# Router and seam of a two-layer graph network with 16 experts: gates from two logits, expert owners ahead of slots, six tiles of weights, square root after block 14

## The chip, the cores and the metric

The kernel runs on one core of a Trainium2 chip. The metric is the device time of the kernel in microseconds (us); of several runs the median counts. The core has five engines that run their own instruction streams in order and meet at semaphores: PE (TensorE, matrix products), DVE (VectorE), ACT (ScalarE), POOL (GpSimd) and SP (SyncE, which here only issues transfers). SP, ACT and POOL issue DMA transfers, which 16 DMA engines carry out.

## The reference, cut to what matters

3125 nodes of 256 features pass four steps, each a layer norm, an operator and a residual: a graph attention with 8 heads, a mixture of 16 experts (top 2), a graph attention of three layers, and a feed-forward block that treats part of the rows. The change lies in the second step:

```python
logits = jnp.einsum('bsd,de->bse', x, gate_w) + gate_b
probs = jax.nn.softmax(logits, axis=-1)
top_probs, top_idx = jax.lax.top_k(probs, 2)
top_probs = top_probs / jnp.sum(top_probs, axis=-1, keepdims=True)
dispatch = jnp.sum(jax.nn.one_hot(top_idx, n_experts, dtype=x.dtype) * top_probs[..., None], axis=-2)
h1 = jnp.einsum('bsd,edh->bseh', x, w1)
h2 = jnp.einsum('bsd,edh->bseh', x, w2)
hidden = jax.nn.silu(h1) * h2
expert_out = jnp.einsum('bseh,eho->bseo', hidden, w3)
return jnp.einsum('bseo,bse->bso', expert_out, dispatch)
```

Since the two probabilities are divided by their sum, the gates of a node depend on the difference of its two best logits alone: with d = second − first, the first gate is 1/(1+exp d) and the second exp d/(1+exp d).

## The kernel before, in words

Nodes lie in NB = 25 blocks of P = 128 (NP = 3200 rows with padding), in NCH = 5 chunks of CH = 5 blocks (CW = 640 rows). All is float32 unless a tile says bfloat16.

**First attention** (to about 980 us). For every chunk, head and source block ACT and DVE make a masked weight matrix, and PE multiplies it (L593, L612). The last chunk's end flows into the seam.

**The seam** (980 to 1056 us). What it does, in order:
- Generators in `endings` and `stats` finish the last chunk; `stats` ends with a square root on ACT (L654) and a reciprocal on DVE (L655), and `rows` makes the five normed blocks b20 to b24 (L660, DVE).
- The router goes over the 25 blocks. PE transposes the normed block (L813), ACT copies it from PSUM (L816), and PE multiplies it by `gate_w` (L818) into one PSUM tile of logits. Inside `tc.manual_schedule` DVE and ACT run in the order in which the code names them, so the place of each call is its place in the queue. After b9 stand the square root and the rows; after b9, b19 and b24 `choice` finds the best two experts of the blocks so far with 13 DVE operations (L775 to L782) behind one that adds the bias (L828). After b15 and b23 `gates` turns the logits of the 10 chosen blocks into gates (L787 to L799: an exponential on ACT and 12 DVE operations) and SP writes them to columns D and D+1 of `xn_d` (L800).
- For the first six transfers of later weights (`later_weights`, L844 and L846) ACT is the issuing engine.
- PE sums the chosen experts over nodes (`ptot`, `pin`, L877, L879). DVE makes running sums (`pre`, L886 to L890), the number of tiles of each expert (`tiles`), their ends (`end`), and from these the place of each pair of node and expert (`where`, `place`, `part`, L905 to L922). From `part` come one-hot tiles `slot` and `give` (L932, L937), which PE multiplies (`pslot`) into a list: for each of the 64 expert tiles, which 128 node-expert pairs stand in it.
- Between these, the last five blocks' gates are finished (L790 to L800); then `owner`, the expert of each tile, is made by a comparison of 1024 elements (`which`, L948), a sum (`own`, L950) and a minimum (L951). `token` (row to gather, L964) and `target` (row to add to, L967) come last.

**The experts** (1056 to 1428 us). MU = 56 tiles run always, up to 8 more if the count needs them. For tile i, SP reads `owner[i]` into a register and loads that expert's w1, w2, w3 (512 KB each, L985, L987, L989); these are in a pool `ew0` of three buffers. POOL gathers 128 rows of `xn_d` with their gates (`xg`, L991). PE transposes them, multiplies by w1 and w2 (L1000), ACT and DVE form `hid` (L1004, L1005), PE multiplies by w3 (`po`, L1008), DVE scales by the gate (`yo`, L1014), and POOL adds the rows into `x_d` with an indirect transfer (L1015). Each of these adds waits until the one before has landed.

**After the experts** ACT loads `x` from `x_d` in five transfers (L1030). POOL issues, in its queue's order, `wr`, `br` (L1046, L1048), the two feed-forward matrices `fw1` and `fw2` of 1 MB each (L1056, L1058) and `fb2` (L1061). The feed-forward bias `b1` (4 KB, 8 x 128) is loaded by POOL into a tile named `rjunk` (L1111), transposed on PE (L1113) and copied by DVE (L1114); a scheduler, not the code's order alone, decides where POOL and PE get these, and the rooms of tiles decide with it. Then DVE and ACT norm the rows (`lengths`, L1126 to L1135; L1143) and PE makes features (L136, L1098).

**The second attention** (1494 to 2402 us) is a long chain of PE products (L1345); its `at<-adj` mask loads (L1330, three of 800 KB at first) are issued ahead by SP. The feed-forward block ends the kernel.

Transfers issued by SP and ACT share eight semaphore lanes; a transfer waits for the one before it on its lane.

Of the kernel before, what the change touches and what calls it, by code (L numbers as in the profile page):

```python
# [13 lines left out]
OP = mybir.AluOpType  # L14
# [70 lines left out]
def network(ctx: ExitStack, tc: tile.TileContext, ins, out, flag):  # L85
# [464 lines left out]
    with tc.tile_pool(name="m0a", bufs=1) as ap, tc.tile_pool(name="m0", bufs=2) as mp, tc.tile_pool(  # L550
# [118 lines left out]
        made, state = [], {}  # L669
        evictions, endings = [], []  # L670
        load(0, range(NCH))
        for u in range(len(units) + LEAD0):
            if u == H * NB:
                nc.scalar.dma_start(gate_w, ins["L0_ffn_gate_w"].rearrange("(k p) e -> p k e", p=P))
                nc.scalar.dma_start(gate_b, spread(ins["L0_ffn_gate_b"], NE))
            if u < len(units):
                dc, h, s = units[u]
                if h == H - 1 and s == 0 and dc + 1 < NCH:
                    load(dc + 1, range(NCH - 1))
                made.append(produce(dc, h, s, state))  # L680
            if u < LEAD0:
                continue
            dc, h, s = units[u - LEAD0]
            if h == 0 and s == 0:
                red = mp.tile([P, H, 2 * CH, C1], F32, name="red", bufs=1)
                total = mp.tile([P, CH, H, C1], F32, name="total")
                others = shared(dc, total)
            if s == 0:
                acc = ps.tile([P, 3, 512], F32, name="acc")
            consume(dc, h, s, made.pop(0), acc)  # L690
            for _ in range(2 if s % 4 == 3 else 1):
                next(others, None)
            if s == NB - 1:
                evictions.append((u + LEAD0, dc, h, acc, red))
                if h % 4 == 3:

                    while next(others, None) == h // 4:
                        pass
                    steps = [finish(dc, red, total, h // 4)]
                    if h == H - 1 and dc < NCH - 1:  # L700
                        steps.append(stats(dc))
                    if h == H - 1 and dc == NCH - 2:
                        steps += [rows(g) for g in range(NCH - 1)]
                    endings += [(u + LEAD0 + 2, e) for e in steps]
                    if h == H - 1 and dc + 1 < NCH:

                        load(dc + 1, [NCH - 1])
            if evictions and u >= evictions[0][0]:
                evict(*evictions.pop(0)[1:])
            if endings and u >= endings[0][0] and u % 2 and next(endings[0][1], None) is None:  # L710
                endings.pop(0)
# [52 lines left out]
        t3, l2, ex = [room_of_x(ex3, F32) for _ in range(3)]  # L764
# [19 lines left out]
        def gates(bs, ex, t3):  # L784

            e = ex[:, bs]
            nc.vector.tensor_sub(e, lg[:, bs], across(best[0], bs))  # L787
            nc.scalar.activation(e, e, AF.Exp)
            yield
            nc.vector.tensor_reduce(den[:, bs], e, AX.X, OP.add)  # L790
            nc.vector.reciprocal(den[:, bs], den[:, bs])
            nc.vector.tensor_mul(e, e, across(den, bs))
            for i in range(2):
                nc.vector.tensor_mul(t3[:, bs], e, one_hot[i][:, bs])
                nc.vector.tensor_reduce(gate[:, bs, i], t3[:, bs], AX.X, OP.add)
            nc.vector.tensor_add(den[:, bs], gate[:, bs, 0], gate[:, bs, 1])
            nc.vector.reciprocal(den[:, bs], den[:, bs])
            for i in range(2):
                nc.vector.tensor_mul(gate[:, bs, i], gate[:, bs, i], den[:, bs])  # L799
            nc.sync.dma_start(xn_d[bs.start * P : bs.stop * P, D:].rearrange("(b p) c -> p b c", p=P),  # L800
                                gate[:, bs])
        with tc.manual_schedule(engines={mybir.EngineType.DVE, mybir.EngineType.Activation}):
# [5 lines left out]
            logits = ps.tile([P, 3, 512], F32, name="acc")[:, 0, : NB * NE].rearrange("p (b e) -> p b e", e=NE)  # L808
            done = 0
            for b in range(NB):  # L810
# [5 lines left out]
                nc.scalar.copy(xt[:, : 2 * P], pt[:, : 2 * P])  # L816
                for k in range(2):
                    nc.tensor.matmul(logits[:, b, :], xt[:, k * P : (k + 1) * P], gate_w[:, k, :],  # L818
                                     start=(b == 0 and k == 0), stop=(k == 1), skip_group_check=True)
                if b in (9, 19, NB - 1):  # L820
                    if b == 9:

                        for e in (ends[-1], rows(NCH - 1)):
                            for _ in e:
                                pass
                    bs = slice(done, b + 1)
                    done = b + 1
                    nc.vector.tensor_add(lg[:, bs, :], logits[:, bs, :],  # L828
                                         gate_b[:, None, :].to_broadcast([P, done - bs.start, NE]))
                    choice(bs, t3, l2)  # L830
                if b in (15, 23):
                    giving = gates(bs, ex, t3)
                    next(giving)
                    next(giving, None)
# [26 lines left out]
    with tc.tile_pool(name="mo", bufs=1) as mo:  # L861
# [7 lines left out]
        with tc.tile_pool(name="mg", bufs=1) as mg, tc.tile_pool(name="mg1", bufs=1, space=PSUM) as ps1, tc.manual_schedule(  # L869
# [11 lines left out]
            giving = gates(slice(20, NB), ex, t3)  # L881
            next(giving)

# [19 lines left out]
            end = running(tiles, mg.tile([P, NE], F32, name="end0"), mg.tile([P, NE], F32, name="end1"), NE)  # L903
            base = mg.tile([P, NE], F32, name="base")
# [19 lines left out]

            pslot = ps1.tile([P, 2, MT], F32, name="pslot")
            pairs = lambda t: t.rearrange("p (q e) -> p q e", e=2)[:, :, None, :]
            for i in range(2):
# [17 lines left out]
            which = mg.tile([P, MT, NE], F32, name="which")  # L945
            nc.gpsimd.iota(which, pattern=[[1, MT], [0, NE]], base=0, channel_multiplier=0,
                           allow_small_or_imprecise_dtypes=True)
            nc.vector.tensor_tensor(which, which, end[:, None, :].to_broadcast([P, MT, NE]), OP.is_ge)  # L948
            own = mg.tile([P, MT], F32, name="own")
            nc.vector.tensor_reduce(own, which, AX.X, OP.add)  # L950
            nc.vector.tensor_scalar(owner, own, float(NE - 1), None, op0=OP.min)  # L951

# [16 lines left out]
        def experts(first, last, ew):  # L969

            with tc.tile_pool(name="ep", bufs=2, space=PSUM) as ps:
                w3_loads = []
                for i in range(first, last):
# [10 lines left out]
                    w1 = ew.tile([P, 2, HID], F32, name="w1")  # L984
                    nc.sync.dma_start(w1, ins["L0_ffn_w1"][ds(e, 1)].rearrange("o (k p) h -> p (o k) h", p=P))  # L985
                    w2 = ew.tile([P, 2, HID], F32, name="w2")
                    nc.sync.dma_start(w2, ins["L0_ffn_w2"][ds(e, 1)].rearrange("o (k p) h -> p (o k) h", p=P))  # L987
                    w3 = ew.tile([P, HID // P, D], F32, name="w3")
# [31 lines left out]
        experts(0, MU, ew0)  # L1020
        early.close()
        count = nc.values_load(used[0:1, 0:1], min_val=0, max_val=MT)
        with tc.If(count > MU):
            with tc.tile_pool(name="ew2", bufs=2) as ew:
                experts(MU, MU + 2, ew)
            with tc.If(count > MU + 2):
                with tc.tile_pool(name="ew3", bufs=3) as ew:
                    experts(MU + 2, MT, ew)
# [1146 lines left out]
```

## Time and profile before

| what | us |
|---|---|
| median of 3 runs | 2539.43 |
| the runs | 2529.86, 2539.43, 2539.63 |
| profiled execution, its own time | 2538.2 |
| span of the profiled execution | 2536.3 |
| PE busy in it | 2199.5 (87%) |
| DVE busy | 1553.2 (61%) |
| ACT busy | 1286.6 (51%) |
| POOL busy | 194.9 (8%) |

The span lies 1.9 us under the execution's own time. A row of a timeline reads: start, length, engine, line, operation, tiles out<-in, shape, count, and in brackets how long the engine had been idle and what it waited for. A row of windows reads: stretch, its length, busy time of each engine with its instructions, the granted share of the TensorE clock, the mean busy share of the 16 DMA engines, and what they moved in GB/s. An engine name with q (SPq, POOLq) means the issuing of a transfer.

### The profile page before, as it was taken

The page shows a single profiled execution, that of the slowest core. Times are in us where ns is not written, and L with a number is a line of the kernel's source. Part 1 is how long each engine was busy: PE and PEld are TensorE (multiplying, and loading weights), DVE is VectorE, ACT ScalarE, POOL GpSimd, SP SyncE. Part 2 cuts the span into 40 slices and gives each one's busy share as a digit, 9 for nine tenths or more (in the row PEclk, how much of TensorE's full clock was granted, in tenths as well). Part 3 has the DMA queues.
Part 4 walks back from the last instruction along what each step waited for, and adds up shares of the span by engine and source line. Part 5 has one row for each costly group of instructions (what it writes and reads, how often), then busy time and mean ns, then how long its engine had stood idle before and what let it go on. Part 6 is the DMA issues. An engine that isn't in the chain of part 4 may idle for free. (4 is left out here: it accounts for less than half of the span.)

```text
span 2536.3 us, 38394 instructions
## 1 busy us (share of the span) xinstructions
PE 2199.5 (87%) x15049; PEld 1872.8 (74%) x15049; DVE 1553.2 (61%) x2978; ACT 1286.6 (51%) x1804; POOL 194.9 (8%) x182
## 2 busy tenths in 40 slices
PE   2526699999999998499999589999899998999997
PEld 1325568888888887488888468888788887888765
DVE  6699979999999997532222334444344443677851
ACT  1364479999999895011111154444444445444321
POOL 2000000000000000233443200000000000000021
PEclk9755599999999998699999799999999999999999
DMA  3005430202020211699999412222122221444330
GB/s 88 12 23 192 130 114 22 92 25 95 22 97 22 66 43 34 205 305 297 279 277 290 130 55 71 71 83 76 58 71 80 73 72 59 107 109 97 70 83 18
DMA packets 155547, 260.80 MB, mean 103 GB/s; under 512 B 12938, under 2 KB 99481, under 8 KB 155353
## 3 DMA queue, kind: packets, MB, share of 16 engines
q1 hardware_dynamic: 127187, 211.13, 26.7%
q0 software_dynamic: 13440, 22.80, 4.3%
q10 hardware_dynamic: 14726, 24.27, 3.3%
q8 instruction: 123, 2.02, 0.3%
q14 instruction: 71, 0.58, 0.1%
HBM read 211.60 MB, written 46.57 MB: 102 GB/s over the span
## 5 line engine op out<-in xcount | busy, mean ns | idle before, releaser
L1345 PE MATMUL bcc<-hx,r 128*128 128x257 f32 x3750 | 840.0, 383 | 13.4 <-DVE r L1336 13.4
L1345 PEld LDWEIGHTS bcc<-hx,r 128*128 128x128 f32 x3750 | 710.9, 191 | 113.0 <-DVE r L1336 13.7
L586 ACT ACTIVATE t<-row,steep 128x640 bf16<-128x640 f32 x800 | 592.4, 817 | 59.2 <-DVE m L588 38.3
L593 PE MATMUL acc<-parts,m 128*128 128x198 bf16 x5000 | 575.3, 247 | 4.6 <-DVE m L588 3.7
L1336 DVE SCALAR_TENSOR_TENSOR r<-t,colc,at 128x640 f32<-128x640 f32 x375 | 329.5, 882 | 397.9 <-PE bcc L1345 384.3
L1334 ACT ACTIVATE t<-rowb,colm,cola 128x640 f32<-128x640 f32 x375 | 341.9, 919 | 387.0 <-DVE r L1336 386.4
L593 PEld LDWEIGHTS <-m 128*128 128x128 bf16 x5000 | 442.2, 96 | 101.7 <-DVE m L588 17.0
L612 PE MATMUL all<-parts,at 128*128 128x396 bf16 x1250 | 366.4, 337 | 6.1 <-DVE total L614 3.8
L588 DVE TENSOR_TENSOR m<-t,at 128x1280 bf16<-128x1280 bf16 x400 | 327.3, 820 | 39.6 <-ACT t L586 31.8
L1000 PEld LDWEIGHTS h<-xT,w 128*128 128x128 f32 x1792 | 214.1, 194 | 17.5 <-ACT xT L138 14.4
L1000 PE MATMUL h<-xT,w 128*128 128x128 f32 x1792 | 219.1, 279 | 7.8 <-ACT xT L138 7.7
L529 PE MATMUL pa<-oh,ol 128*128 128x100 bf16 (+1 forms) x1120 | 94.7, 277 | 111.9 <-DVE oh L522 111.9
L579 DVE SCALAR_TENSOR_TENSOR m<-row,nleft,at 128x640 bf16<-128x640 f32 x200 | 174.7, 874 | 10.5 <-DMA adj<-cnt 8.0
L529 PEld LDWEIGHTS <-ol 128*128 128x128 bf16 x1120 | 87.0, 141 | 119.5 <-DVE oh L522 62.0
L1004 ACT ACTIVATE hid<-h 128x512 f32<-128x512 f32 x56 | 33.4, 597 | 261.0 <-PE h L1000 256.1
L1014 DVE TENSOR_SCALAR yo<-po,share 128x256 f32<-128x256 f32 x56 | 27.1, 484 | 203.0 <-DMA x_d<-yo,target 123.8
L612 PEld LDWEIGHTS <-at 128*128 128x128 bf16 x1250 | 119.2, 98 | 16.2 <-issue 10.7
L1008 PE MATMUL po<-w,hid 128*128 128x256 f32 x448 | 113.2, 396 | 18.5 <-DVE hid L1005 18.4
L532 ACT CAST cnt<-pa 128x2000 bf16<-128x2000 f32 x40 | 73.0, 1826 | 82.8 <-PE pa L529 82.8
L138 ACT COPY xT<-pt 128x256 f32<-128x256 f32 x158 | 56.0, 375 | 107.1 <-PE pt L136 104.0
L1008 PEld LDWEIGHTS po<-w,hid 128*128 128x128 f32 x448 | 82.0, 193 | 35.2 <-DVE hid L1005 22.5
L1015 POOL DMA_INDIRECT x_d<-yo,target x56 | 89.5, 1599 | 213.4 <-DVE share L1010 121.9
(410 smaller groups left out, 1740.6 us busy)
## 6 DMA issues: line engine op xcount, KB each, us to landing
w<-in_L_ffn_w_dram SPq DMA_DIRECT2D x168, 512.0 KB
at<-adj SPq DMA_DIRECT2D x100, 800.0 KB
adj<-cnt SPq DMA_DIRECT2D x10, 2000.0 KB
row<-er_d ACTq DMA_DIRECT2D x40, 320.0 KB
xf_d<-hx SPq DMA_DIRECT2D x5, 1282.5 KB
right<-rr_d ACTq DMA_DIRECT2D x15, 320.0 KB
x_d<-x SPq DMA_DIRECT2D x5, 640.0 KB
xn_d<-at SPq DMA_DIRECT2D x5, 640.0 KB
```

The costliest lines, as they stand in the source:

```text
L529: nc.tensor.matmul(pa[:, q // NW, p0 + c0 : p0 + c1], hot[0][:, q // 2, :, q % 2], hot[1][:, q // 2, c0:c1, q % 2], start=(u == 0), stop=( ...
L579: nc.vector.scalar_tensor_tensor(m, row, nleft[:, s, h : h + 1], at[:, k, :], op0=OP.is_ge, op1=OP.mult)
L586: nc.scalar.activation(t[:, int(i), :], row, AF.Relu, bias=steep[:, s, h : h + 1], scale=STEEP)
L588: nc.vector.tensor_tensor(m, t, at[:, k - 1 : k + 1, :], OP.min)
L593: nc.tensor.matmul(acc[:, db // 2, db % 2 * C6 : (db % 2 + 1) * C6], m[:, db * P : (db + 1) * P], parts[:, s, h, :], start=(s == 0 and db ...
L612: nc.tensor.matmul(alone, at, parts[:, s, hs, 3 * C1 :], start=(s == 0), stop=(s == NB - 1))
L1000: nc.tensor.matmul(ph[:, f, :], w[:, k, f * P : (f + 1) * P], xt[:, k, :], start=(k == 0), stop=(k == 1))
L1008: nc.tensor.matmul(po, hid[:, f, :], w3[:, f, :], start=(f == 0), stop=(f == HID // P - 1))
L1015: nc.gpsimd.indirect_dma_start(out=x_d, out_offset=bass.IndirectOffsetOnAxis(ap=target[:, i : i + 1], axis=0), in_=yo, in_offset=None, com ...
L1334: nc.scalar.activation(t, rowb[:, dw], AF.Relu, bias=colm[:, s : s + 1], scale=cola[:, s : s + 1])
L1336: nc.vector.scalar_tensor_tensor(r, t, colc[:, s : s + 1], at[:, s % CH, :], op0=OP.add, op1=OP.mult)
L1345: nc.tensor.matmul(accs[dc][db][:, : D + 1], r[:, db * P : (db + 1) * P], hx[:, s, : D + 1], start=(s == 0), stop=(s == NB - 1))
```

## The change

Four edits meet in the seam.
- **Router.** Two steps (b0 to b14, b15 to b24) in two PSUM banks take the place of three in one; square root and rows stand after b14 instead of b9.
- **Gates.** `gates` goes. The exponential of the difference of the two best logits is taken once for all 25 blocks; an addition, a reciprocal and a product follow once `part` is made, and ACT writes all gates in one transfer of 3200 pieces of 8 bytes.
- **Owners.** `used`, `which`, `own` and `owner` stand right behind `end`, ahead of `base`.
- **Weights.** w1, w2, w3 get six buffers each.

```diff
-            logits = ps.tile([P, 3, 512], F32, name="acc")[:, 0, : NB * NE].rearrange("p (b e) -> p b e", e=NE)
-            done = 0
+            logits = ps.tile([P, 3, 512], F32, name="acc")
+            steps = (0, 15, NB)
...
-                if b in (9, 19, NB - 1):
-                    if b == 9:
-                        for e in (ends[-1], rows(NCH - 1)):
+                if b == 14:
+                    for e in (ends[-1], rows(NCH - 1)):
...
-                if b in (15, 23):
-                    giving = gates(bs, ex, t3)
-                    next(giving)
-                    next(giving, None)
+            nc.vector.tensor_sub(den, best[1], best[0])
+            nc.scalar.activation(gate[:, :, 1], den, AF.Exp)
...
-            giving = gates(slice(20, NB), ex, t3)
-            next(giving)
...
             end = running(tiles, mg.tile([P, NE], F32, name="end0"), mg.tile([P, NE], F32, name="end1"), NE)
+            nc.vector.tensor_copy(used, end[:, NE - 1 :])
+            which = mg.tile([P, MT, NE], F32, name="which")
...
+            nc.vector.tensor_scalar(owner, own, float(NE - 1), None, op0=OP.min)
             base = mg.tile([P, NE], F32, name="base")
...
             nc.vector.tensor_copy(part[:, :, :, :NB], part_i)
+            nc.vector.tensor_scalar(den, gate[:, :, 1], 1.0, None, op0=OP.add)
+            nc.vector.reciprocal(gate[:, :, 0], den)
+            nc.vector.tensor_mul(gate[:, :, 1], gate[:, :, 1], gate[:, :, 0])
+            nc.scalar.dma_start(xn_d[:, D:].rearrange("(b p) c -> p b c", p=P), gate)
...
-            next(giving, None)
-            nc.vector.tensor_copy(used, end[:, NE - 1 :])
...
-            nc.vector.tensor_scalar(owner, own, float(NE - 1), None, op0=OP.min)
             second = mg.tile([P, MT], F32, name="second")
...
-                    w1 = ew.tile([P, 2, HID], F32, name="w1")
+                    w1 = ew.tile([P, 2, HID], F32, name="w1", bufs=deep)
...
-        experts(0, MU, ew0)
+        experts(0, MU, ew0, 6)
```

The diff also hands the tiles `red` and `total` of the first attention out from a function; the stream of instructions there stays the same. Outside the diff the scheduler places two things anew, as the built order of instructions shows: `at<-adj` (three loads on SP) stands amid the experts' weight loads instead of ahead of them, and `rjunk` (POOL) stands behind `fw1`, `fw2` and `fb2` instead of among the first gathers, so that PE's transpose of it and DVE's copy of it come first on PE, and ahead of the reciprocal L1130 on DVE, after the experts.

More of the change, by code (lines that the diff above doesn't have):

```diff
@@ L669, in network, with sums_of @@
         made, state = [], {}
+        def sums_of(dc):
+            return mp.tile([P, H, 2 * CH, C1], F32, name="red", bufs=1), mp.tile([P, CH, H, C1], F32, name="total")
+        red, total = sums_of(0)
         evictions, endings = [], []
@@ L684, in network @@
             if h == 0 and s == 0:
-                red = mp.tile([P, H, 2 * CH, C1], F32, name="red", bufs=1)
-                total = mp.tile([P, CH, H, C1], F32, name="total")
+                if dc:
+                    red, total = sums_of(dc)
                 others = shared(dc, total)
@@ L763, in network @@
         nc.vector.tensor_copy(tritb, trit)
-        t3, l2, ex = [room_of_x(ex3, F32) for _ in range(3)]
+        t3, l2 = [room_of_x(ex3, F32) for _ in range(2)]
         assert taken[0] <= (NCH - 1) * CH * D
@@ L782, in choice @@
             nc.vector.tensor_mul(chosen[:, bs], chosen[:, bs], across(real, bs))
[L784 to L801, printed above, removed]
         with tc.manual_schedule(engines={mybir.EngineType.DVE, mybir.EngineType.Activation}):
@@ L903, in network @@
             end = running(tiles, mg.tile([P, NE], F32, name="end0"), mg.tile([P, NE], F32, name="end1"), NE)
+            nc.vector.tensor_copy(used, end[:, NE - 1 :])
+            which = mg.tile([P, MT, NE], F32, name="which")
+            nc.gpsimd.iota(which, pattern=[[1, MT], [0, NE]], base=0, channel_multiplier=0,
+                           allow_small_or_imprecise_dtypes=True)
+            nc.vector.tensor_tensor(which, which, end[:, None, :].to_broadcast([P, MT, NE]), OP.is_ge)
+            own = mg.tile([P, MT], F32, name="own")
+            nc.vector.tensor_reduce(own, which, AX.X, OP.add)
+            nc.vector.tensor_scalar(owner, own, float(NE - 1), None, op0=OP.min)
             base = mg.tile([P, NE], F32, name="base")
@@ L941, in network @@
                                      start=(i == 0 and b == 0), stop=(i == 1 and b == NB - 1))
-            next(giving, None)
-            nc.vector.tensor_copy(used, end[:, NE - 1 :])
[L945 to L951, printed above, removed]
             second = mg.tile([P, MT], F32, name="second")
@@ L967, in network, with experts @@
             nc.vector.scalar_tensor_tensor(target, number, -1.0, none2, op0=OP.add, op1=OP.add)
-        def experts(first, last, ew):
+        def experts(first, last, ew, deep):
             with tc.tile_pool(name="ep", bufs=2, space=PSUM) as ps:
@@ L1024, in network @@
             with tc.tile_pool(name="ew2", bufs=2) as ew:
-                experts(MU, MU + 2, ew)
+                experts(MU, MU + 2, ew, 2)
             with tc.If(count > MU + 2):
                 with tc.tile_pool(name="ew3", bufs=3) as ew:
-                    experts(MU + 2, MT, ew)
+                    experts(MU + 2, MT, ew, 3)
         for g in range(NCH):
```

23 lines of the change are left out of this document (13 added, 10 removed).

## The prediction

> **What bounds the kernel now.** First I read the busy rows by windows around the seam.
>
> ```profile
> 975.00:990.00 15.00, 13.31 (x119) 11.25 (x116) 10.06 (x25) 3.85 (x11) 0.00 (x0) 1.00 0.05 19
> 990.00:1004.00 14.00, 11.44 (x52) 10.22 (x53) 10.21 (x36) 5.32 (x13) 0.00 (x0) 0.50 0.22 75
> 1004.00:1020.00 16.00, 7.80 (x37) 6.99 (x37) 10.90 (x41) 2.36 (x7) 1.57 (x2) 0.50 0.48 98
> 1020.00:1047.00 27.00, 6.17 (x52) 5.32 (x50) 25.31 (x66) 0.00 (x0) 0.00 (x0) 0.55 0.22 83
> 1047.00:1062.00 15.00, 6.38 (x30) 5.87 (x31) 2.01 (x11) 2.62 (x4) 8.31 (x9) 0.54 0.89 302
> 1062.00:1415.00 353.00, 326.77 (x2324) 300.40 (x2322) 87.90 (x241) 50.51 (x109) 133.84 (x102) 0.99 0.94 281
> ```
>
> Busy columns are PE, PEld, DVE, ACT, POOL; then clock, DMA share, GB/s. Until 1020 the router shares the path with DVE at half the clock; from 1020 to 1047 DVE is busy 25.31 of 27 us, so every operation taken from its chain counts; 1047 to 1056 is the first gather. Then PE works 93% of the experts' stage: there nothing but PE's rate and the chain of scatter-adds counts. Next the timeline, where the seam hands over and where the experts end:
>
> ```profile
> 990.94 0.30 ACT L654 ACTIVATE grstd<-gmv,eps 128x5 f32<-128x5 f32 x1 [2.36 <-DVE gmv L653]
> ...
> 1020.22 0.57 DVE L886 COPY pre<-ptot 128x400 f32<-128x400 f32 x1 [0.61 <-PE ptot L877]
> ...
> 1046.05 0.20 DVE L951 TENSOR_SCALAR owner<-own 128x64 int32<-128x64 f32 x1
> ...
> 1047.05 0.42 SPq L985 DMA_DIRECT2D w<-in_L_ffn_w_dram  x1
> ...
> 1047.76 1.04 POOL L991 DMA_INDIRECT xg<-xn_d,token  x1 [36.14 <-DVE none L966]
> ...
> 1055.05 0.60 POOL L1111 DMA_DIRECT2D rjunk<-in_L_ffn_b_dram  x1
> ...
> 1055.55 1.09 PE L136 MATMUL pt<-ident,xg 128*128 128x128 f32 x4 [11.55 <-DMA xg<-xn_d,token]
> ```
>
> ```profile
> 1430.87 0.76 POOL L1056 DMA_DIRECT2D fw<-in_L_ffn_w_dram  x1
> ...
> 1432.51 0.60 POOL L1061 DMA_DIRECT2D fb<-in_L_ffn_b_dram  x1
> ...
> 1437.33 0.19 DVE L1130 RECIPROCAL rstd<-rstd 128x5 f32<-128x5 f32 x1 [1.81 <-ACT rstd L1128]
> ...
> 1439.13 0.69 PE L136 MATMUL pt<-ident,rows 128*128 128x128 f32 x2 [20.79 <-DVE rows L1143]
> ```
>
> Last, the list of transfers with their median time to landing:
>
> ```profile
> fw<-in_L_ffn_w_dram POOLq DMA_DIRECT2D x2, 1024.0 KB, 15.1
> ...
> fb<-in_L_ffn_b_dram POOLq DMA_DIRECT2D x1, 128.0 KB, 14.7
> rjunk<-in_L_ffn_b_dram POOLq DMA_DIRECT2D x1, 4.0 KB, 6.0
> ```
>
> **The change part by part** (lines of before). The order of instructions is the same up to 988 us.
>
> *Square root and router.* Before, the square root (L654) waits on ACT from 988.58 to 990.94, and b10's copy behind it. After, b10 to b14 are copied first. At full clock a block costs 0.69 us (copies at 982.0 and 988.21, nine blocks); after 989.9, at a clock of 0.50, 1.29 (b12's copy at 994.62, b23's at 1008.77: eleven blocks in 14.15). I let the clock fall as before: b10, b11 at 0.7, b12 to b14 at 1.29, so b14's copy ends at 993.7. Square root, reciprocal and five rows take 2.3 us (990.94 to 993.2 before), so DVE is free at 996.0. The choice is 14 operations: 0.275 us each on 80 elements (1015.78 to 1019.61), 0.36 on 160 (993.13 to 998.09), so an estimate of 0.445 on 240: 6.2 us, to 1002.2. b15 to b24 run beside it and end at 993.7 + 10 × 1.29 + 1 = 1007.6; 14 × 0.36 = 5.05 gives 1012.7, and `pre` starts 0.6 later, **1013.3 against 1020.22: −6.9**. The third choice (3.85) and the exponentials' waits (1.73, 2.14) are what goes.
>
> *Owners and gates.* Behind `end` (5.89 us after `pre` starts) the owner's group moves in front: 1043.48 to 1046.16, 2.7 us. Behind `part` come three gate operations on 25 elements, 0.22 each as the 10-wide rows L791 and L797: 0.65. Gone from behind the slots are the last gates (1041.03 to 1043.48) and that group. But both hid PE's `pslot` (1041.17 to 1044.0), which is now bare for 3.0 us. So from `pre` to the gather: before 27.5 us (1020.22 to 1047.76); after 11.3 + 2.7 + 0.65 + 9.5 (slots) + 3.0 + 1.6 (`second` to gather) = 28.75. The gather is issued at **1042.1: −5.7**; SP's first load at 1013.3 + 5.9 + 2.7 + 0.8 = 1022.7 instead of 1047.05.
>
> *The gates' one write.* Issued about 1028 on ACT. The first gather waits for it, and so does SP's twelfth weight load, which stands on the same lane. Eleven loads, 5.8 MB at 350 to 370 GB/s (what 990 to 991 moved, and the experts' peak), last until 1039. The 1280-piece writes took 1 us alone and about 3 beside other loads, so 3200 pieces take 2.5 to 7.5 us: 1030.5 to 1035.5, hidden. If each piece waited behind a packet of weights (0.2 us, from the `as` and `ad` loads' 48 packets per engine in 10 us), it would land once the eleven loads end, about 1041; it can't be later, since the twelfth is held. Cost 0, at most +2. The Trainium skill, "DMA: Bandwidth & Descriptors", section "Queues, rings and completion order", says each DMA engine takes turns between queue rows a packet at a time, 9 to 17 descriptors; by that the 200 pieces of an engine need some 12 to 22 turns and the cost is 0 as well.
>
> *First gather to PE.* Before 7.8 us, against three to eight loads just issued; the list has 5.5 as the median landing and 2.8 as the least. After, the early tiles' weights are in place. I take 6: PE starts at 1048.1, **−7.5** (bounds −5 to −10).
>
> *Six tiles in flight.* In the steady stage no wait names weights; PE's gaps there are `hid` behind scatter-adds. Gain 0. Early, the `as`/`ad` products held DVE from 1081 to 1089 (a PE gap of 3.2): the transfers may land sooner, 0 to −3; I take −1. The three mask loads (2.4 MB, free at 1016 before) move into the stage: 2.4 MB at 281 GB/s is 8.5 us of transfer, bounds 0 to +4, I take +0.5, since PE has six tiles ahead.
>
> *The hidden part: `rjunk`.* The bigger weights took its room. Its load now follows `fw1`, `fw2`, `fb2` and three iotas on POOL, issued about 1433.6 instead of 1055.05. Its PE transpose leads PE's queue, and its copy stands ahead of L1130 on DVE. Behind waits everything: the reciprocal, rows, all 25 feature blocks, then the 900 us attention. `fb2`, one place ahead on the same queue, landed at 1432.51 + 14.7 = 1447.2; so `rjunk` lands near 1447.5, and the reciprocal starts at 1448.2 instead of 1437.33: **+10.8**. The other end is its own 6.0 us: 1439.6, +2.5. I take +10.5, by the neighbour in its queue. Nothing covers it: PE idles 20.79 us there already, and the features run back to back until 1487.
>
> *Sum* against the profiled 2538.2 (1.2 under the median 2539.43): −7.5 − 1 + 0.5 + 10.5 = +2.5, **2540.7**; I say 2541.
>
> **The clock in the router** is the place where row and rule part. The clock went to 0.50 at 989.9, when PE had been idle for 0.4 us only, and stayed there for 54 us. The Trainium skill, "TensorE: Matmul & The Clock Gate", section "What's actually happening", says the gate watches free-running windows of 3.4 us, halving after an idle and releasing after a busy one; PE's idle time from 989.5 to 991.5 goes with this change, so by the rule the clock could stay full and the sum would be that of the first rival below. But the rows have PE busy for 3.5 of the 4 us up to 990 and the clock down all the same, so I keep the drop.
>
> **The rivals.**
> 1. *Full clock in the router.* b24 ends near 999.5, the first choice at 1000.3, the second at 1005.3, `pre` at 1005.9: another −7.4. 2533.5. For it: the same rhythm ran at 1.00 from 983 to 989. Against it: the drop itself.
> 2. *`rjunk` costs nothing much*: eight rows of 512 bytes slip through. 2540.7 − 8 to −10.5 = 2531, and with a full clock 2524, faster. For it: in the experts' traffic it took only 6.0 us. Against it: `fb`'s 14.7 in the same queue at the same place.
> 3. *Slower: the scatter chain.* Scatter-adds follow each other's landing, median 5.8 us, 6.5 a tile; PE needs about 6.0. If deeper weights and mask loads keep the transfers fuller, each landing grows. It decides from 0.25 us a tile on: 56 × 0.25 = 14, 2555. For it: DMA share 0.94 in the stage, and an early landing without traffic 4.5 instead of 5.8. Against it: SP still loads just what PE frees.
> 4. *The change doesn't do what it says*: the gather waits for the gates' write instead of the slots, to 1044 or 1048. 2543 to 2547.
>
> **How the numbers follow.** A measurement tells about 0.5%, 12.7 us, from no change: faster is below 2526.7, slower above 2552.1. Forecast 0.50 (2536 to 2546), rival 1 0.17, rival 2 0.14 (of it 0.04 with full clock), rival 3 0.12, rival 4 0.07. Faster: 0.04 and the low tails of rivals 1 and 2, 0.10. Slower: rival 3 and a tail of 4, 0.13. Same: 0.77. The range from 2526 to 2553 leaves out rival 2 with full clock and the upper half of rival 3.
>
> **What would show it.** `pre` at 1013 and the gather at 1042 confirm the seam; a clock of 1.00 from 990 to 1005 is rival 1. Weights from 1023, gates landed before 1041. Then after the last scatter, `rjunk` landing near 19 us after it, DVE's reciprocal and PE's first `pt` 10 us later than before: scatter end to `pt` 11.2 us before, 22 after. If that is 11 to 14, rival 2 holds. A mean scatter period over 6.7 is rival 3. I am wrong altogether if the first 980 us move.

## The result and the profile after

The changed kernel took 2547.11 us (median of 7 runs, 2540.32 to 2551.61), the kernel before 2533.39 (median of 7, 2525.06 to 2539.63). The ratio is 1.0053, 95% interval 1.0033 to 1.0073: slower by 8 to 18 us, where I had forecast 2541 and +2.5 against the profiled run. The range (2526 to 2553) held the time; it lies just above the band that I had called likeliest (2536 to 2546), and the ratio just beyond 0.5%. The profiled execution after has a span of 2549.8 us against 2536.3, so 13.5 us are to be found. Both profiled executions lie some 5 us above their kernel's median (2551.61 over 2547.11, 2538.2 over 2533.39).

Where they are, by marks read from both traces (us from the span's start):

| mark | before | after | difference |
|---|---|---|---|
| first product of the first attention | 332.87 | 335.14 | +2.27 |
| router, first copy | 982.00 | 985.01 | +3.01 |
| `pre` starts | 1020.22 | 1019.84 | −0.38 |
| first gather issued | 1047.76 | 1049.96 | +2.20 |
| PE's first transpose of the experts | 1055.55 | 1056.10 | +0.55 |
| reload of x issued | 1428.28 | 1425.98 | −2.30 |
| first transpose of rows | 1439.13 | 1447.55 | +8.42 |
| copy of the sixth feature block | 1453.87 | 1466.34 | +12.47 |
| first product of the second attention | 1493.80 | 1506.86 | +13.06 |

The first 3.0 us come before the first changed instruction. I take them as chance, which moves the first mark by several us from run to run (330.6 to 335.1 in the fourteen profiles of this study). The seam and the experts give 5.3 back; the 10.7 and 4.1 us that follow are the loss.

The windows of the kernel after, in the stretches shown for before (PE, PEld, DVE, ACT, POOL; clock, DMA share, GB/s):

```profile
975.00:990.00 15.00, 13.79 (x114) 12.06 (x113) 9.63 (x16) 5.15 (x11) 0.00 (x0) 0.88 0.00 1
990.00:1004.00 14.00, 13.91 (x71) 13.51 (x71) 6.60 (x25) 4.50 (x13) 0.00 (x0) 0.50 0.15 51
1004.00:1020.00 16.00, 10.93 (x53) 10.18 (x52) 9.39 (x28) 4.49 (x10) 1.57 (x2) 0.50 0.40 120
1020.00:1047.00 27.00, 5.73 (x51) 5.32 (x50) 22.95 (x54) 0.00 (x0) 0.00 (x0) 0.50 0.64 211
1047.00:1062.00 15.00, 4.44 (x23) 4.07 (x24) 2.67 (x15) 2.06 (x4) 7.61 (x8) 0.52 0.80 244
1062.00:1415.00 353.00, 326.53 (x2324) 301.00 (x2322) 87.91 (x241) 51.03 (x110) 133.97 (x102) 0.99 0.92 275
```

PE is busy for 13.91 of 14 us in the router, no stall is left there, and the clock is at 0.50 all the same. DVE's share of 1020 to 1047 fell from 25.31 to 22.95, and DMA moved 211 GB/s instead of 83: weights now run there. PE's work in the 353 us of experts is the same to 0.3 us.

The timeline of the kernel after at the seam (its lines are 9 to 14 lower than before's from L813 on, the moved owner group aside):

```profile
1019.84 0.57 DVE L872 COPY pre<-ptot 128x400 f32<-128x400 f32 x1 [0.57 <-ACT x L823]
...
1028.30 0.19 DVE L898 TENSOR_SCALAR owner<-own 128x64 int32<-128x64 f32 x1
...
1029.29 0.40 SPq L976 DMA_DIRECT2D w<-in_L_ffn_w_dram  x1
...
1034.50 0.45 ACTq L924 DMA_DIRECT2D xn_d<-x  x1
...
1047.95 0.22 DVE L955 SCALAR_TENSOR_TENSOR token<-number,none 128x64 int32<-128x64 f32 x1
...
1049.18 0.37 SPq L980 DMA_DIRECT2D w<-in_L_ffn_w_dram  x1
1049.96 0.99 POOL L982 DMA_INDIRECT xg<-xn_d,token  x1 [33.67 <-DMA xn_d<-x]
...
1056.10 0.66 PE L136 MATMUL pt<-ident,xg 128*128 128x128 f32 x2 [9.29 <-DMA xg<-xn_d,token]
```

The bracket of the gather is the thing to see: before, it had waited for DVE; now its releaser is the transfer of the gates (`xn_d<-x`), issued at 1034.50 and landed near 1049. SP's twelfth weight load, at 1049.18, was let go by the same landing.

And after the experts:

```profile
1430.06 0.74 POOL L1047 DMA_DIRECT2D fw<-in_L_ffn_w_dram  x1
...
1431.70 0.58 POOL L1052 DMA_DIRECT2D fb<-in_L_ffn_b_dram  x1
...
1432.65 0.57 POOL L1102 DMA_DIRECT2D rjunk<-in_L_ffn_b_dram  x1
...
1435.50 0.30 ACT L1119 ACTIVATE rstd<-mv,eps 128x5 f32<-128x5 f32 x1
...
1445.41 0.24 PE L1104 MATMUL ph<-ident,rjunk 8*128 8x8 f32 x1 [28.40 <-DMA rjunk<-in_L_ffn_b_dram]
1445.69 0.17 DVE L1105 COPY fb<-ph 128x8 f32<-128x8 f32 x1 [11.58 <-PE ph L1104]
1445.77 0.18 DVE L1121 RECIPROCAL rstd<-rstd 128x5 f32<-128x5 f32 x1
...
1447.55 0.69 PE L136 MATMUL pt<-ident,rows 128*128 128x128 f32 x2 [1.90 <-DVE rows L1134]
```

```profile
fb<-in_L_ffn_b_dram POOLq DMA_DIRECT2D x1, 128.0 KB, 13.4
rjunk<-in_L_ffn_b_dram POOLq DMA_DIRECT2D x1, 4.0 KB, 12.6
```

ACT has the root ready at 1435.8. DVE could take it at once, but its queue has the copy of the bias ahead, and that waits for 4 KB which take 12.6 us to land behind 2 MB.

### The profile page after: what moved, and what is told of

The parts are those of the page before. It is cut to its first block, busy times and chain, and to the rows that moved or that the text cites. A ratio compares the mean times of both kernels' runs of the same rounds, so it can differ in the third digit from the quotient of the medians.

```text
span 2549.8 us, 38337 instructions
## 1 busy us (share of the span) xinstructions
PE 2207.5 (87%) x15049; PEld 1881.4 (74%) x15049; DVE 1543.5 (61%) x2932; ACT 1286.1 (50%) x1802; POOL 194.0 (8%) x182
## 4 chain that ended last, share of the span: by engine, by line
PE 45%; DMA 10%; DVE 7%; ACT 2%; issue 2%; POOL 0%; ACTq 0%; DVEq 0%; POOLq 0%
PE bcc L1336 29%; DMA x_d<-yo,target 8%; PE ph L1089 3%; PE h L991 2%; PE acc L593 2%; PE bcc L1395 2%; PE po L999 1%; PE bcc L1388 1%; PE all L612 1%; DVE r L1327 1%; DVE rjunk L1198 1%; PE acc L807 1%; PE pt L136 1%; DVE yo L1005 1%; DMA xn_d<-x 1%
## 5 line engine op out<-in xcount | busy, mean ns | idle before, releaser
L1336 PEld LDWEIGHTS bcc<-hx,r 128*128 128x128 f32 x3750 | 711.1, 191 | 113.2 <-DVE r L1327 13.7
L593 PEld LDWEIGHTS <-m 128*128 128x128 bf16 x5000 | 442.1, 96 | 102.9 <-DVE m L588 18.1
L991 PEld LDWEIGHTS h<-xT,w 128*128 128x128 f32 x1792 | 214.1, 194 | 17.1 <-ACT xT L138 13.9
L579 DVE SCALAR_TENSOR_TENSOR m<-row,nleft,at 128x640 bf16<-128x640 f32 x200 | 174.2, 872 | 10.5 <-DMA adj<-cnt 8.1
L999 PE MATMUL po<-w,hid 128*128 128x256 f32 x448 | 113.9, 399 | 18.8 <-DVE hid L996 18.8
```

Source lines behind the costliest of these rows:

```text
L579: nc.vector.scalar_tensor_tensor(m, row, nleft[:, s, h : h + 1], at[:, k, :], op0=OP.is_ge, op1=OP.mult)
L593: nc.tensor.matmul(acc[:, db // 2, db % 2 * C6 : (db % 2 + 1) * C6], m[:, db * P : (db + 1) * P], parts[:, s, h, :], start=(s == 0 and db ...
L991: nc.tensor.matmul(ph[:, f, :], w[:, k, f * P : (f + 1) * P], xt[:, k, :], start=(k == 0), stop=(k == 1))
L999: nc.tensor.matmul(po, hid[:, f, :], w3[:, f, :], start=(f == 0), stop=(f == HID // P - 1))
L1336: nc.tensor.matmul(accs[dc][db][:, : D + 1], r[:, db * P : (db + 1) * P], hx[:, s, : D + 1], start=(s == 0), stop=(s == NB - 1))
```

## The experiments

Theory A: the bias load behind `fw1` and `fw2` is the loss, the seam is worth some us. Rival B: the seam and the deeper weights themselves cost, and the bias wait is covered by the reload of x. All ratios below are to the kernel before on the same chip, with 95% intervals; the medians of before in the three groups of runs were 2534.34, 2535.39 and 2533.84.

**1. Bias early.**

```diff
+    fb1 = lw.tile([P, FH // P], F32, name="fb1")
+    nc.gpsimd.dma_start(fb1, ins["L1_ffn_b1"].rearrange("(f p) -> p f", p=P))
...
-        b1r = gw.tile([P, NP - CW], BF16, name="rjunk").bitcast(F32)[:NF, :P]
-        nc.gpsimd.dma_start(b1r, ins["L1_ffn_b1"].rearrange("(f p) -> f p", p=P))
-        pr = ps.tile([P, 512], F32, name="ph")
-        nc.tensor.transpose(pr[:, :NF], b1r, ident[:NF, :NF])
-        nc.vector.tensor_copy(fb1, pr[:, :NF])
```

> The changed kernel, but the 4 KB feed-forward bias is loaded in the seam straight into its final tile (no tile rjunk, no transpose on PE, no copy on DVE). Theory A (the bias load behind 2 MB is what costs): the first transpose of rows follows the last scatter-add's landing by 11 to 12 us instead of 21.6, so -8 to -10 there, and the features come out of the half clock some 4 us cheaper; in all -11 to -14 us against the changed kernel, ratio to the kernel before 0.999 to 1.002. Theory B (the seam and the deeper weights cost, the bias is covered by the reload of x): at most -4 us, ratio 1.003 or more.

Measured 2533.24, ratio 1.0005 (0.9989 to 1.0020). The timeline of this kernel after the experts:

```profile
1423.49 3.90 ACTq L1023 DMA_DIRECT2D x<-x_d  x5
...
1432.62 0.19 DVE L1117 RECIPROCAL rstd<-rstd 128x5 f32<-128x5 f32 x1 [1.74 <-ACT rstd L1115]
...
1434.67 0.66 PE L136 MATMUL pt<-ident,rows 128*128 128x128 f32 x2 [20.24 <-DVE rows L1130]
```

From the reload's issue to the first transpose 11.2 us (10.85 before, 21.6 after). A holds: the medians differ by 13.9 us. The load's new place alone undoes the whole loss.

**2. Six buffers alone**, in the kernel before (`bufs=deep` with 6, as in the change, and nothing else).

> The kernel before with one part of the change alone: six buffers for w1, w2, w3. The bias load moves behind the two 1 MB loads here too. Theory A: the first transpose of rows comes 8 to 10 us later after the last scatter-add than before (19.5 to 21.5 instead of 11.2), and in all +9 to +14 us: ratio 1.0035 to 1.0055. Theory B: six buffers are neutral or gain at the start of the experts, 0 to -3 us: ratio 0.999 to 1.000.

Measured 2554.03, ratio 1.0077 (1.0053 to 1.0101), above what A expected. Reload to first transpose 21.6 us: A's mechanism comes from the deeper pool alone. But the loss is larger than A alone allows: the experts' stage itself (first transpose to reload) took 382.9 us instead of 372.7. Seven of its early scatter-adds in a row (the fourth to the tenth interval) stand 7.7 to 8.2 us apart, in the kernel before 5.7 to 8.0: without early owners the eighteen first loads, issued from 1045.0 to 1078.6, run beside the first tiles. That these loads are the reason was not tried by itself. So depth has a price of its own, which the next runs divide.

**3. Three buffers**, the rest of the change kept (`experts(0, MU, ew0, 3)`).

> The changed kernel with three buffers for the weights as before; the bias load stands among the first gathers again, and the mask loads ahead of the experts. Theory A: the whole loss goes, -11 to -14 us against the changed kernel, and what the seam gains or loses is left: ratio 0.998 to 1.001. Theory B (the seam itself costs): ratio 1.003 or more.

Measured 2524.20, ratio 0.9960 (0.9940 to 0.9981), better than either theory had it. All side effects go, and the seam's edits are seen to gain some 10 us. Against run 1 it is better by 9 us, which the bias can't explain. Two things differ: the gather and the mask loads. First the gather, in the timeline of run 3:

```profile
1045.87 0.22 DVE L955 SCALAR_TENSOR_TENSOR token<-number,none 128x64 int32<-128x64 f32 x1
1046.42 0.99 POOL L982 DMA_INDIRECT xg<-xn_d,token  x1 [34.08 <-DVE none L957]
...
1049.30 0.66 PE L136 MATMUL pt<-ident,xg 128*128 128x128 f32 x2 [4.58 <-DMA xg<-xn_d,token]
```

and in that of run 1, where six buffers let SP issue eleven loads before the gates have landed:

```profile
1039.76 0.23 DVE L957 SCALAR_TENSOR_TENSOR token<-number,none 128x64 int32<-128x64 f32 x1
...
1042.95 0.37 SPq L982 DMA_DIRECT2D w<-in_L_ffn_w_dram  x1
1043.72 1.02 POOL L984 DMA_INDIRECT xg<-xn_d,token  x1 [34.56 <-DMA xn_d<-x]
...
1048.75 0.66 PE L136 MATMUL pt<-ident,xg 128*128 128x128 f32 x2 [10.14 <-DMA xg<-xn_d,token]
```

Token to PE takes 3.4 us in run 3 and 9.0 in run 1: 4.0 of wait for the gates instead of 0.5, and a gather of 5.0 beside weights instead of 2.9 alone.

**4. Gates early**: the three operations and the write stand ahead of `fullt`, the first line of the tile counts.

> The changed kernel, but the three gate operations and the one gate write stand ahead of the tile counts, so that the write is issued some 4 us ahead of the first weight load instead of 5 us behind it. Theory C (the first gather waits for the gate write, which takes turns with the weights): the write lands before 1030, the gather follows the token without the 2 us it now waits, the twelfth weight load is not held for 10 us; first gather -1.5 to -2.5 us against token, in all 0 to -4 us against the changed kernel. Rival: the write lands as late, because weights go first: no change. Theory A is untouched by it: the loss at the bias stays, ratio 1.003 to 1.005.

Measured 2540.38, ratio 1.0023 (1.0007 to 1.0038), somewhat better than expected. The write was issued at 1022.4, 5.6 us ahead of the first weights, and the gather followed its token after 0.50 us, released by DVE. Theory C holds for the wait; 6.7 us between the medians is more than the 1.5 that the wait measures in the profiles of the changed kernel and of this one, and the intervals of the two ratios (1.0033 to 1.0073 and 1.0007 to 1.0038) overlap. The gather still took 6.3 us, since the twelfth to eighteenth load now run beside it.

**5. Masks behind the weights**, on top of run 1: an order of issue is asked for, after the reload of x.

```diff
+                        if layer == 0 and dc == 0 and s < 3 * CH:
+                            tc.add_manual_dep(
+                                load.ins, back.ins.name,
+                                mybir.DependencyInfo(mybir.DependencyClass.NoSync, mybir.DependencyReason.SCHED_ONLY),
+                                reason="masks behind the reload")
```

> The changed kernel with the early bias load, and besides the three mask loads (at, 800 KB each) held until the reload of x is issued, so that they no longer run amid the experts' weights. Theory D (the three mask loads cost 5 to 8 us in the experts' stage, since the scatter-adds behind each land 1 to 3 us later): scatter 5 to scatter 20 takes 102 to 104 us instead of 107 to 109, and in all -4 to -8 us against the early bias load alone: ratio to the kernel before 0.997 to 0.999. Theory E (the six-deep weights themselves slow the scatter-adds): scatter 5 to 20 stays at 107 to 109, ratio 1.000 to 1.002.

Measured 2528.48, ratio 0.9966 (0.9949 to 0.9983): 4.8 us under run 1 by the medians, 10 by the ratios, whose intervals do not touch. The request sets only SP's order, so the masks were issued when SP had sent its last weights, at 1378, not behind the reload itself. The stretch from scatter-add 5 to 20 in the windows of the kernel before, after, and of run 5:

```profile
1105.00:1207.00 102.00, 95.63 (x696) 88.40 (x694) 24.57 (x65) 16.07 (x35) 38.23 (x30) 1.00 0.99 303
```

```profile
1104.00:1211.00 107.00, 100.18 (x714) 92.43 (x713) 25.75 (x67) 15.41 (x33) 37.68 (x29) 0.98 0.99 304
```

```profile
1102.00:1203.00 101.00, 98.09 (x711) 90.84 (x710) 25.00 (x66) 16.06 (x35) 38.05 (x29) 1.00 1.01 307
```

Fifteen tiles take 102, 107 and 101 us at the same 303 to 307 GB/s: the DMA engines are full (share 0.99 to 1.01), so what is loaded besides in the stretch (two of the three masks and the start of the third, some 1.6 MB by these rows) pushes the scatter-adds back. Three kernels with the masks in this stretch (the changed one, runs 1 and 4) needed 107 to 109. D holds against E in this stretch: without the masks there six buffers needed 101 and 98 (runs 5 and 10), three buffers 95 to 104. Run 2, with six buffers, late owners and no masks there, needed 106, so the masks aren't the only thing that lengthens it. In the trace of the changed kernel the masks are issued at 1140.6, 1164.2 and 1206.3, and the scatter-adds around the first two stand 8.6, 8.2 and 9.3 us apart.

**6. Warm router**: three buffers, and four idle products per block, whose results are not used.

```diff
+                for _ in range(4):
+                    nc.tensor.matmul(logits[:, 2, :P], tritb, tritb, start=True, stop=True, skip_group_check=True)
```

> The changed kernel with three buffers, and four idle bfloat16 products (128x128 by 128x128, result unused) per router block, so that PE has more to do in the router. Theory F (the router's own rhythm, with its two 16-column products a block, lets the clock fall to 0.50 within 1 to 8 us): with the idle products the clock stays at 1.00 from 980 to 1000, a block costs 0.7 to 0.9 us instead of 1.17, the last copy comes 17 to 22 us after the first instead of 27.5, and in all -4 to -8 us against three buffers alone: ratio 0.993 to 0.995. Rival (the clock falls because of the wait at the router's start, before the idle products help): the blocks run at 0.50 as before and the idle products cost: 0 to +8 us.

Measured 2533.26, ratio 0.9972 (0.9946 to 0.9997), 9 us over run 3 by the medians. Theory F falls. The windows of this run:

```profile
982.00:984.00 2.00, 1.29 (x12) 1.06 (x13) 1.93 (x5) 0.65 (x2) 0.00 (x0) 1.00 0.00 0
984.00:985.00 1.00, 1.00 (x11) 0.99 (x11) 1.00 (x2) 0.24 (x1) 0.00 (x0) 0.80 0.00 0
985.00:1017.00 32.00, 31.91 (x205) 31.20 (x204) 13.78 (x41) 7.79 (x22) 0.00 (x0) 0.50 0.12 42
```

The clock falls two us after the first copy and stays at 0.50 for 32 us in which PE is busy for 31.91; a block costs 1.5 us instead of 1.17, and the router 35.8 instead of 27.5.

**7. Owners late**: three buffers, and the owner group back behind the slots.

> The changed kernel with three buffers and the owner group back behind the slots, as before. Theory G (owners ahead of slots gain by having the first weights in place, so that the first gather lands in 3 us instead of 7.8, and the group's 2.7 us hides PE's second pslot either way): the first transposes of the experts start 4 to 5 us later than with three buffers alone, ratio 0.997 to 0.998. Rival (weights are not late, the first gather alone decides): no change, 0.996.

Measured 2527.76, ratio 0.9972 (0.9952 to 0.9991), 3.6 us over run 3 by the medians, with intervals that overlap. In the profile the gather's 7.6 us to PE are back (2.9 in run 3), while the token follows `pre` 2.7 us sooner (by 25.4 us instead of 28.1). In sum PE's first transpose of the experts follows the router's first copy by 67.8 us instead of 66.1: later by 1.7, or 2.0 without the router's part, where G had said 4 to 5. The mechanism of G is in the rows, its size is not, and the difference of the times alone doesn't prove it.

**8. Warm features**: three buffers, and four products of 512 columns of the reloaded x, unused, ahead of `lengths(0)`.

```diff
+        warm = ps.tile([P, 512], F32, name="ph")
+        for _ in range(4):
+            nc.tensor.matmul(warm, ident, x[:, 0:2, :].rearrange("p b c -> p (b c)"), start=True, stop=True)
```

> The changed kernel with three buffers, and four idle products of 512 columns of x ahead of the first transposes of rows after the experts, between the landing of x and the first rows. Theory H (the clock stays at 0.50 in the first features because PE stood idle for 20 us, and that costs 4 us): full clock from the first or second block on, the sixth block's copy comes 9 us after the first instead of 10.5 to 15.5, in all -1 to -4 us: ratio 0.9945 to 0.9955. Rival (the features' rhythm sets the clock): no change or +1.

Measured 2521.32, ratio 0.9925 (0.9900 to 0.9951; four runs). From the first transpose of rows to the sixth copy it took 12.9 us instead of 13.7 in run 3. The measure that H named, from the first copy to the sixth, did not reach its 9 us: 10.9, in run 3 10.5. The time gained more than the profile explains; run 11 tries it alone.

**9. The parts put together**: three buffers, gates early, warm features.

> The changed kernel with three buffers, the gates' operations and write ahead of the tile counts, and the four idle products ahead of the features: the version put together from the runs so far. Three buffers gave 0.996 and the idle products 0.9925; with three buffers the gather was held only 0.5 us by the gates' write, so the early write should add 0 to -1 us: ratio 0.992 to 0.995. If the warm features' gain was mostly chance (their own profile shows about 1 us of it), 0.995 to 0.996.

Measured 2520.03 (2519.69 to 2525.66), ratio 0.9948 (0.9933 to 0.9963): the best median of the study, though its interval overlaps those of run 3 (0.9940 to 0.9981) and run 8 (0.9900 to 0.9951). In this profile the features fell back to half clock in spite of the warm-up:

```profile
1420.00:1430.00 10.00, 7.29 (x24) 4.20 (x22) 6.66 (x28) 2.38 (x10) 0.00 (x0) 0.84 1.01 354
1430.00:1436.00 6.00, 4.97 (x13) 3.23 (x12) 3.10 (x12) 1.67 (x5) 0.00 (x0) 0.50 0.11 38
```

**10. Six buffers, mended**: run 5 with the gates early.

> The changed kernel with six buffers and all three side effects mended: early bias load, mask loads behind the reload, gates' write ahead of the weights. Theory I (six buffers gain nothing once their side effects are gone): the gather follows the token at once instead of 4 us later, ratio 0.995 to 0.997, no better than three buffers alone (0.996). Rival (depth helps the scatter chain through the stage): 0.993 or less.

Measured 2529.05, ratio 0.9974 (0.9961 to 0.9986). The gather follows its token after 0.51 us, the bias and the masks are out of the way, and it is no better than three buffers (run 3, 0.9960; I had expected 0.995 to 0.997). Theory I holds: in sum six buffers gain nothing that can be measured.

**11. Warm features in the kernel before**, nothing else.

> The kernel before with the four idle products ahead of the features and nothing else. Theory H (half clock in the first features): -1 to -4 us, ratio 0.9985 to 0.9995, and the sixth feature block's copy 9 to 10.5 us after the first instead of 11.5. Rival: no change, 1.000 or above.

Measured 2531.00, ratio 0.9989 (0.9976 to 1.0001): −2.8 us by the medians, not clear of no change. The sixth copy came 11.0 us after the first, where H had 9 to 10.5; before it was 11.5. H isn't shown.

**12. Square root at block 9** again: three buffers, `if b == 9`, two choices.

> The changed kernel with three buffers, square root, reciprocal and rows back after block 9 instead of 14; the choices stay in two. Theory J (the place of the square root is worth the wait that ACT has there, 2.4 us in the profile before, and nothing at half clock, when block 9 comes later than the statistics): 0 to +2 us against three buffers alone, ratio 0.996 to 0.997. Rival (it was the main gain of the router): +3 us or more, ratio 0.9975 or above.

Measured 2525.39, ratio 0.9962 (0.9948 to 0.9977), as run 3. Theory J holds: the new place of the root is worth nothing that can be measured.

## Why the prediction was right, and where it was not

The range held because the largest term was there and of the right size. Of the difference I had a small part only: +2.5 against 13.7 by the medians. That the time itself came out just 6 us from mine is luck in part, since the three runs of before that I started from had a median 6 us above that of the seven (2539.43, 2533.39). Point by point:

- **The bias.** I took +10.5, from 10.8 by `fb`'s row; reload to first transpose grew from 10.85 to 21.57, **+10.7**. Its neighbour `fb` in POOL's queue was the right row to price it by (14.7 forecast from before, 12.6 measured; it was issued 1 us sooner than I had put it). What failed here is what I said follows: "the features run back to back until 1487". They ran, but at half clock until 1467.6 instead of 1447.3, and from the first transpose to the sixth copy took 18.8 us instead of 14.7: **+4.1 that my sum did not have**. All three profiles with the late bias (after, runs 2 and 4) show 18.1 to 18.8; of the eleven others run 6 has 18.2, run 9 has 16.7, and nine have 12.9 to 14.8. So the late bias goes with a long half clock, though not it alone. What holds the clock there stays open: in the changed kernel PE was busy for 13.39 of 16 us at 0.50,

```profile
1448.00:1464.00 16.00, 13.39 (x34) 8.21 (x33) 7.85 (x33) 4.76 (x16) 0.00 (x0) 0.50 0.00 1
1464.00:1468.00 4.00, 3.96 (x12) 2.93 (x13) 2.21 (x9) 1.20 (x4) 0.00 (x0) 0.55 0.01 3
```

  and in run 1 it was let go at about 1441, 6.4 us after the first transpose, with PE less busy (first row mixed, second full):

```profile
1434.00:1442.00 8.00, 5.89 (x15) 3.81 (x16) 5.60 (x22) 2.21 (x7) 0.00 (x0) 0.56 1.03 364
1442.00:1450.00 8.00, 6.66 (x30) 4.41 (x30) 5.29 (x21) 3.71 (x12) 0.00 (x0) 1.00 0.27 92
```

- **Mask loads.** I took +0.5, bounds 0 to +4, "since PE has six tiles ahead". Weights ahead don't help: the scatter-adds share the DMA engines, and those were full. By run 5 the masks cost 5 us (medians) to 10 (ratios), and in the two profiles scatter-adds 5 to 20 take 107.4 us instead of 101.7. This term was mis-sized, and its upper bound too low. My own figure, 8.5 us of transfer time at 281 GB/s, was the nearest row, and I argued it away.
- **The gates' write.** I took 0, at most +2. In the changed kernel the write landed near 1049, 14.5 us after its issue, and the gather waited 1.5 us more than where it isn't held (0.50 us behind its token). In runs 1 and 5 it waited 3.5 and 4.0 more. The mechanism was rival 4's; that rival 4's 2547 is also the measured time is luck, for its wait had been priced at 2 to 6 us. Two sizes were wrong. The eleven loads ended some 18 us after the first was issued, not 16.3, since DMA moved only 212 GB/s from 1029.0 to 1034.5. And the write itself, which I had put at 2.5 to 7.5 us, went piece by piece beside the weights. The queues of the changed kernel from 1038 to 1047 (packets, MB, share of the DMA engines; q1 carries the weights, q10 the write):

```profile
q1 hardware_dynamic: 2205, 3.27, 96.7%
q10 hardware_dynamic: 2184, 0.02, 13.7%
```

  That is one piece of 8 bytes for one packet of weights; the last 1032 packets of the write moved from 1047 to 1049, when the weights were through. This is the condition that I had named and not taken ("if each piece waited behind a packet of weights"). Alone, in run 4, the whole write moved in 2.0 us. Both 1280-piece writes of the kernel before moved in 0.9 us; I had put the second at about 3. The estimate from the Trainium skill's turns between queue rows ("DMA: Bandwidth & Descriptors", "Queues, rings and completion order"), cost 0, differs from the measurement too: the write ended only after the weights ahead of it.
- **The router's clock.** I let it fall at 989.9, 7.9 us after the first copy, from one profile. It fell at 986.3, 1.3 us after the first copy:

```profile
984.00:986.00 2.00, 1.00 (x7) 0.77 (x8) 1.97 (x5) 0.65 (x2) 0.00 (x0) 1.00 0.00 0
986.00:987.00 1.00, 1.00 (x9) 1.00 (x9) 0.97 (x3) 0.37 (x1) 0.00 (x0) 0.64 0.00 0
987.00:1004.00 17.00, 16.91 (x87) 16.51 (x85) 9.46 (x30) 5.41 (x15) 0.00 (x0) 0.50 0.12 42
```

  In all fourteen profiles it fell, ten times 1.3 to 2.7 us after the first copy and four times 7.9 to 8.1 (before, runs 1, 8 and 9), and had not come back by 1004. So rival 1, full clock, is refuted, and the length of the changed router depends on chance: from the first copy to `pre` it took 30.2 to 30.3 us in the three changed kernels with the late fall, and 34.2 to 34.8 in the others but run 6 with its idle products. I had 31.3 (982.0 to 1013.3), the late fall carried over from before; the profiled execution had the early one and took 34.8, **+3.5**. In the kernel before it took 38.2 to 38.5 with either. The rule of the Trainium skill that I weighed ("TensorE: Matmul & The Clock Gate", "What's actually happening") would have kept the clock up, since PE has no idle gap there. The measurement decides against it: PE is busy for 16.91 of 17 us at 0.50.
- **The seam.** −7.5 for PE's start; in the profile −2.5 from the router's first copy to PE's first transpose (73.5 to 71.1). Gather to PE, 6, measured 6.1. The chain from `pre` to `token` is 28.1 us; I had 28.75 to the gather itself, as it stands without the wait for the gates (28.1 + 0.5). What was missing is the router's 3.5 us and the gates' 1.5. With three buffers the whole gain shows, 66.1 us, −7.4, but by another sum than mine: the router took 34.6 to `pre` there too, and the gather reached PE in 2.9 us instead of the 6 that I had. That the figure agrees is luck.
- **Six tiles in flight.** Gain 0: right as a sum (run 10), for a reason that I did not see. The last 35 scatter-adds (20 to 55) take 210 to 212 us in the five profiles with six buffers and no mask loads that late (after, runs 1, 4, 5, 10), and 213 to 221 in the eight with three. That gain of some 5 us is spent at the start: from the router's last copy to PE's first transpose it is 41.8 to 43.8 us in those five, and 37.5 to 39.0 in the five with three buffers and early owners, for the first gather waits for the gates or runs beside the extra loads, 5.0 to 6.3 us instead of 2.9. The −1 at the `as` and `ad` loads did not come; PE's gap there is 3.0 us in the changed kernel and 3.2 before.
- **Rivals.** 2 (bias covered) is refuted by the timeline and run 1. 3 (scatter chain slower through the stage) did not decide: the whole chain from scatter-add 0 to 55 took 353.6 us, before 356.6; slower was only the stretch with the mask loads.

The sum by stages, from the two profiles, forecast and measured: up to the router's first copy 0 and +3.0; from there to PE's first transpose −7.5 and −2.5; the experts −0.5 and −2.9; reload to first transpose +10.5 and +10.7; to the sixth copy 0 and +4.1; the rest 0 and +1.0. So the seam and the half clock in the features are where most of the missing 11 us went. In the experts two wrong terms cancelled, which is luck: scatter-adds 5 to 20 took 5.6 us longer, the mask term, and scatter-adds 20 to 55 6.3 us less, the gain that I had put at 0. Single profiles carry chance of several us, in the first row above all.

## What to carry to other kernels

A deeper pool is paid for in places that the diff doesn't name: look at what the room was used for, and where the displaced loads now stand in their queue. A small load in an in-order queue waits for the large ones ahead of it (here 4 KB behind 2 MB took 12.6 us to land), and whatever stands behind its use waits too; issuing it long before took the whole loss away (run 1). When DMA is full in a stage, price every load moved into it by its whole transfer time (here 8.5 us by the rate, 5 to 10 measured), and take the clock's phase from several profiles, never from one.

## What the runs showed of the hardware that I had not expected

The clock stayed at 0.50 for 17 to 32 us while PE's rows were busy for 99% of the time (987 to 1004 after; 985 to 1017 in run 6, with idle products added). A first gather of 128 rows reached PE in 2.9 to 3.0 us where three buffers and early owners had the weights loaded ahead, in 5.0 to 6.3 beside the extra loads of six buffers with early owners, and in 6.4 to 7.8 where the first weights were issued less than 1.1 us ahead of it. And a write of 3200 pieces of 8 bytes, which took 2.0 us alone, took some 10 us beside weight loads, one piece for one packet of 1 or 2 KB.
